# The last three output pairs of an attention kernel: another PSUM room, one sum on another engine, and two products in halves

## The chip, the cores and the metric

The kernel runs on one core of a Trainium2 chip. The metric is the device time of one execution in microseconds, as the median of several runs. PE is TensorE (PEld its weight loads), DVE is VectorE, ACT is ScalarE, POOL is GpSimd, SP is SyncE, which only issues DMAs here.

## The reference, cut to what matters

One multi-query attention layer over 64 blocks of 128 tokens, with a residual: layer norm, queries of 16 heads, one shared key and value, a bias and a causal and key mask, softmax, the output projection `Wo`, a second layer norm with gain `g_out`, and `x` added.

```python
B, H, N, DH, DIM = 64, 16, 128, 64, 512
xn   = layernorm(x, g_in)
q    = (xn @ Wq) -> [B, H, N, DH] * DH**-0.5
k, v = xn @ Wkv, each with a null row ahead
sim  = q @ k.T + bias, masked
out  = softmax(sim) @ v -> [B, N, H * DH]
out  = out @ Wo                      # 1024 -> 512
x    = x + layernorm(out, g_out)
```

All arithmetic is fp32.

## The kernel before, in words

The order of all instructions is written out by hand (`manual_schedule`); each engine has its own queue in that order, and semaphores for true dependencies are put in when the program is built. Blocks are handled in pairs. A step `d` makes the scores of blocks `a = 2d` and `b = 2d + 1`, takes the values and the output of the pair `p = 2d - 2, p + 1`, and normalises the pair before that, `l`.

The output projection of a pair is done with seven products instead of eight (a Strassen-like scheme over the two blocks and the two halves of `Wo`). `out_sum(p, k)` makes four sums of the transposed attention outputs `oT` (128 x 512 each): k = 0 writes the tile `yS`, the other three write over parts of `oT` in place. So sum 1 must wait until product 1 has read its operand, and sum 3 until product 2 has. `out_product(p, k, ...)` makes product k with 4 matmuls of 128 x 128 by 128 x 256 into one PSUM tile; products 6, 7 and 4 add to what product 1 left in its tile, product 3 to what product 5 left. `out_keep` copies a tile in between (`yp1`, `yu2`, `yp5`), `out_part` writes a half block of the output `ys` (256 columns).

Steps 1 to 29 are `turn` and `body`. The two steps ahead of the last pair, d = 30 and 31, are `turn_end` and `body_end`; `turn_end(32)` and `body_last` then finish the last pair, blocks 62 and 63, which has no scores beside it.

- `turn_end(d)`: scores of `a` and `b`, adding them to the bias (`scores_add`), maxima, the values of the pair `p` (`values`, tile `po`), ScalarE's exponentials of the first half of `a`, then `values_out_one`, which adds the null value and moves `po` to `oT`, ScalarE (L759) and VectorE (L757) in turn. The reciprocal `rinv(a, 0)` and the last `scores_add` follow on VectorE.
- `body_end(d)`: sums on GpSimd (L806), products on TensorE (L823) in the order 1, 2, 6, 5, 7, 3, 4, and among them the softmax of `a` and `b`: `scores_max`, `exps` (ScalarE), `rinv` (VectorE), `scale` (GpSimd, L664), `blocks_T` (VectorE transposes).
- `late_stats`, `pair_pow`, `late_nmr`, `late_norm`, `late_gain`, `late_residual` normalise a finished block: statistics on VectorE, the power -0.5 on GpSimd (L867), a scaling on ScalarE (L1037), the gain on VectorE (L1040), the residual on GpSimd (L1043), which also issues the store.
- `body_last`: products 1, 2, 5, 6, 3, 7, 4 of the last pair, and the normalisation of blocks 59 to 63. For block 62 VectorE subtracts the mean and multiplies by the gain (L1148) and then scales and adds the residual in one instruction (L1155). For block 63 `last_stats` reads product 4 out of PSUM.

PSUM has four kinds of room: `ps_s` "s" is one tile of two banks that the scores of `(a, 1)` use, `ps_q` "a" and "c", `ps_y` "X" and "Y", and `ps_w` "w" (two of it). Product 1 of a pair lies in "a" in `body_end`, and in "c" in `body_last`. The values `po` of the pair use "a", "w", "Y" and "w".

Of the kernel before, what the change touches and what calls it, by code (L numbers as in the profile page):

```python
# [17 lines left out]
def kernel(  # L18
# [63 lines left out]
    P = 128  # L82
# [593 lines left out]
    def blocks_T(b, lo=0, hi=R8):  # L676

        if lo == 0:
            sbs[b] = hp.tile([P, 6, R8, Q], FP, tag="sb", name=f"sb_{b}")
        nc.vector.transpose(  # L680
            sbs[b][:, :, lo:hi].rearrange("p j e q -> p e j q"),
            S[b][:, lo:hi, 1 : ROW - 1].rearrange("p e (j k) -> p e j k", k=Q),
        )
# [107 lines left out]
        p, m = ((e12, e11), (e22, wT[:, 0]), (e22, e12), (e21, wT[:, 1]))[k]  # L791
        nc.gpsimd.tensor_tensor(wT[:, k], p, m, ALU.subtract)

    def out_sum(p, k):

        h11, h12 = oT[p][:, 0], oT[p][:, 1]
        h21, h22 = oT[p + 1][:, 0], oT[p + 1][:, 1]
        if k == 0:
            yS[p] = bp.tile([P, HC, N], FP, tag="yS", name=f"yS_{p}", bufs=1)
        o, a, b, op = (  # L800
            (yS[p], h21, h22, ALU.add),
            (h11, yS[p], h11, ALU.subtract),
            (h21, h22, h11, ALU.subtract),
            (h12, h12, h11, ALU.subtract),
        )[k]
        nc.gpsimd.tensor_tensor(o, a, b, op)  # L806

    def out_product(p, k, pool, tag, start=True):
        key = "y" + tag
        if start:  # L810
            prod[key] = pool.tile([P, HE], FP, tag=tag, name=f"py{tag}_{p}_{k}")
        a, b = oT[p], oT[p + 1]
        h, w = {
            1: (a[:, 0], e11),
            2: (a[:, 1], e21),
            3: (a[:, 1], e22),
            4: (b[:, 1], wT[:, 3]),
            5: (yS.get(p), wT[:, 0]),
            6: (a[:, 0], wT[:, 1]),
            7: (b[:, 0], wT[:, 2]),  # L820
        }[k]
        for c in range(HC):
            nc.tensor.matmul(  # L823
                prod[key],
                h[:, c, :],
                w[:, c, :],
                start=(start and c == 0),
                stop=(c == HC - 1),
                skip_group_check=not start,
            )  # L830
# [8 lines left out]
    def out_part(b, e, tag, name=None):  # L839
        if b not in ys:  # L840
            if B - 6 <= b < B - 2:
                ys[b] = gp.tile(
                    [P, DIM], FP, tag=f"xS{b - B + 7}", name=f"y_{b}", bufs=1
                )
            elif b == B - 1:
                ys[b] = gp.tile([P, DIM], FP, tag="xT", name=f"y_{b}")
            else:
                ys[b] = hp.tile([P, DIM], FP, tag="y", name=f"y_{b}", bufs=3)
        o = ys[b][:, lo_e if e == 0 else hi_e]
        if name is None:  # L850
            nc.scalar.copy(o, prod["y" + tag])
        else:
            nc.vector.tensor_tensor(o, prod["y" + tag], kept.pop(name), ALU.add)
# [12 lines left out]
    def pair_pow(b):  # L866
        nc.gpsimd.tensor_tensor(yn[b][1], yn[b][1], nhalf, ALU.pow)  # L867
# [66 lines left out]
    def turn_end(d):  # L934

        a, b, p = 2 * d, 2 * d + 1, 2 * d - 2
        if d == PAIRS:
            blocks_T(*late_T.pop())
            late_gain(p - 4)
            late_residual(p - 4, nc.gpsimd)  # L940
            late_nmr(p - 3)
            values_rooms_apart(p)
            result_room(p)
            for m in (p, p + 1):
                values(m)
# [24 lines left out]
        scores_add(b, 1)  # L970

    def body_first():
# [66 lines left out]
    def late_gain(b):  # L1039
        nc.vector.tensor_tensor(ys[b], ys[b], gob, ALU.mult)  # L1040
# [5 lines left out]
    def body_end(d):  # L1046

        a, b, p, l = 2 * d, 2 * d + 1, 2 * d - 2, 2 * d - 4
        last = d + 1 == PAIRS
        lo, hi = (0, R8 // 2), (R8 // 2, R8)  # L1050
        for r in range(p, B if last else p + 2):
            load_res(r)
        out_sum(p, 0)
        scores_max(a, 1)
        late_stats(l if last else l + 1)
        out_product(p, 1, ps_q, "a")
        exps(b, 0, 0, 4)
        out_keep("a", "yp1", "yp1")
# [11 lines left out]
        out_keep("a", "yu2", "yu2")  # L1070
        exps(a, 1, *lo)
        rinv(a, 1, *lo)
        scale(a, 1, *lo)
        out_sum(p, 3)
        late_nmr(l)
        out_product(p, 5, ps_y, "Y")
        exps(a, 1, *hi)
        rinv(a, 1, *hi)
        scale(a, 1, *hi)
        out_keep("Y", "yp5", "yp5")  # L1080
        blocks_T(a, *lo)
        if last:
            late_stats(l + 1)
        else:
            late_nmr(l + 1)
        out_product(p, 7, ps_q, "a", start=False)
        exps(b, 1, *lo)
        out_part(p + 1, 1, "a", "yp5")
        rinv(b, 1, *lo)
        scale(b, 1, *lo)  # L1090
        blocks_T(a, *hi)
        out_product(p, 3, ps_y, "Y", start=False)
        exps(b, 1, *hi)
        rinv(b, 1, *hi)
        scale(b, 1, *hi)
        out_part(p, 1, "Y", "yu2")
        late_norm(l)
        if last:
            pair_pow(l + 1)
        else:  # L1100
            late_norm(l + 1)
        blocks_T(b, *lo)
        late_T.append((b, *hi))
        out_product(p, 4, ps_q, "a", start=False)
        out_part(p + 1, 0, "a")
        if not last:
            for m in (l, l + 1):
                late_gain(m)
                late_residual(m, nc.gpsimd)

    def body_last():
# [1 line left out]
        p = B - 2  # L1113
        y = p - 2
        st = [
            small.tile([P, 2, 6], FP, tag=f"stl{i}", name=f"stl{i}", bufs=1)
            for i in range(2)
        ]
# [28 lines left out]
        mv, rstd = last_stats(p, st[0], (1, ys[p][:, hi_e]))  # L1147
        nc.vector.scalar_tensor_tensor(  # L1148
            ys[p], ys[p], mv[:, 0:1], gob, ALU.subtract, ALU.mult
        )  # L1150
# [10 lines left out]
        y = ys[p + 1]  # L1161
# [374 lines left out]
```

## Time and profile before

| | us |
|---|---|
| median of 3 runs | 1038.36 |
| lowest and highest run | 1037.15, 1039.06 |
| the profiled execution's own time | 1036.99 |
| its span in the profile | 1035.2 |

The span runs from the first to the last recorded instruction of the profiled execution; the time of an execution also has 1.8 us around it. In the profile a row names line, engine, operation and tiles (out<-in). A bracket at the end of a timeline row says how long the engine sat idle before it and what ended that. Step 30 begins at 974.25 us of the span, step 31 at 993.73, and the last pair at 1013.24.

### The profile page before, as it was taken

The page shows a single profiled execution, that of the slowest core. Times are in us where ns is not written, and L with a number is a line of the kernel's source. Part 1 is how long each engine was busy: PE and PEld are TensorE (multiplying, and loading weights), DVE is VectorE, ACT ScalarE, POOL GpSimd, SP SyncE. Part 2 cuts the span into 40 slices and gives each one's busy share as a digit, 9 for nine tenths or more (in the row PEclk, how much of TensorE's full clock was granted, in tenths as well). Part 3 has the DMA queues.
Part 4 walks back from the last instruction along what each step waited for, and adds up shares of the span by engine and source line. Part 5 has one row for each costly group of instructions (what it writes and reads, how often), then busy time and mean ns, then how long its engine had stood idle before and what let it go on. Part 6 is the DMA issues. An engine that isn't in the chain of part 4 may idle for free.

```text
span 1035.2 us, 31163 instructions
## 1 busy us (share of the span) xinstructions
PE 1022.7 (99%) x12337; PEld 902.3 (87%) x12337; DVE 772.4 (75%) x1629; ACT 680.4 (66%) x2709; POOL 726.7 (70%) x540
## 2 busy tenths in 40 slices
PE   9999999999999999999999999999999999999997
PEld 8888888888888888888888888888888888888876
DVE  6776777876777877778777778767778777767687
ACT  4756677666677566686666776666776666856582
POOL 4897767676676767758667676776767677576686
PEclk9999999999999999999999999999999999999999
DMA  7514152241613315133151522415233151330211
GB/s 216 158 36 147 63 166 78 68 126 63 180 69 104 96 63 177 62 125 106 42 167 62 163 79 65 133 63 176 72 104 96 60 180 63 112 89 25 85 63 63
DMA packets 69226, 105.12 MB, mean 102 GB/s; under 512 B 9044, under 2 KB 33496, under 8 KB 67288
## 3 DMA queue, kind: packets, MB, share of 16 engines
q1 hardware_dynamic: 68640, 102.47, 31.7%
q8 instruction: 97, 1.59, 0.6%
q10 hardware_dynamic: 440, 0.66, 0.2%
q14 instruction: 49, 0.40, 0.1%
HBM read 67.45 MB, written 35.65 MB: 100 GB/s over the span
## 4 chain that ended last, share of the span: by engine, by line
PE 96%; POOL 2%; DMA 1%; issue 0%; DVE 0%; ACT 0%; ACTq 0%; POOLq 0%; DVEq 0%
PE pa L534 20%; PE pyX L823 19%; PE pyY L823 10%; PE pc L534 10%; PE po L740 8%; PE pkv L350 6%; PE pyw L823 5%; PE pw L534 5%; PE ps L611 3%; PE pq L469 3%; PE sc_X L611 2%; PE sc_Y L611 2%; PE sc_a L611 1%; POOL oT L806 1%; PE pya L823 1%; PE sc_w L611 1%
## 5 line engine op out<-in xcount | busy, mean ns | idle before, releaser
L642 ACT ACTIVATE s<-s,nmax 128x65 f32<-128x65 f32 (+1 forms) x1024 | 372.0, 367 | 59.0 <-DVE nmax L633 59.0
L664 POOL TENSOR_TENSOR s<-s,rinv 128x512 f32<-128x512 f32 (+1 forms) x132 | 190.8, 1447 | 166.0 <-DVE rinv L660 166.0
L576 POOL TENSOR_TENSOR s<-biasp,mneg 128x1552 f32<-128x1552 f32 (+1 forms) x65 | 206.0, 3172 | 41.2 <-DVE s L626 32.8
L642 ACT ACTIVATION_READ_ACCUMULATOR s<-s,nmax 128x1 f32 x1024 | 194.3, 190 | 0.0
L823 PE MATMUL pyX<-wT,oT 128*128 128x256 f32 x696 | 164.4, 379 | 0.0
L680 DVE STREAM_TRANSPOSE sb<-s 128x1536 f32<-128x1536 f32 (+1 forms) x68 | 114.1, 1678 | 61.5 <-POOL s L664 61.5
L823 PEld LDWEIGHTS pyX<-wT,oT 128*128 128x128 f32 x696 | 132.1, 190 | 18.1
L633 DVE TENSOR_REDUCE nmax<-s 128x8 f32<-128x1032 f32 (+1 forms) x128 | 121.4, 949 | 0.1
L534 PE MATMUL pa<-xS,wq 128*128 128x256 f32 x472 | 121.1, 379 | 0.0
L552 ACT COPY qT<-pa 128x256 f32<-128x256 f32 x59 | 22.0, 373 | 149.3 <-PE pa L534 149.2
L534 PEld LDWEIGHTS pa<-xS,wq 128*128 128x128 f32 x472 | 89.5, 190 | 12.3
L277 POOL TENSOR_TENSOR rstd<-rstd,nhalf 128x1 f32<-128x1 f32 x64 | 35.6, 557 | 77.2 <-DVE rstd L276 77.2
L806 POOL TENSOR_TENSOR oT<-oT 128x512 f32<-128x512 f32 x64 | 80.5, 1277 | 3.7 <-PE pyw L823 1.4
L740 PE MATMUL po<-sb,vr 32*64 32x256 f32 (+1 forms) x4008 | 81.4, 303 | 0.0
L740 PEld LDWEIGHTS po<-sb,vr 32*64 32x64 f32 x4008 | 71.2, 130 | 8.1 <-issue 5.7
L555 DVE TENSOR_TENSOR qT<-pc,ku 128x256 f32<-128x256 f32 x118 | 49.0, 415 | 38.5 <-ACT ku L546 21.3
L759 ACT ACTIVATE oT<-po,nv 128x512 f32<-128x512 f32 (+1 forms) x127 | 73.7, 654 | 1.2 <-PE po L740 1.1
L546 ACT COPY ku<-pa 128x256 f32<-128x256 f32 x118 | 43.9, 372 | 40.6 <-PE pa L534 37.4
L350 PE MATMUL pkv<-wkv,xT 128*128 128x128 f32 x512 | 65.2, 281 | 0.0
L350 PEld LDWEIGHTS pkv<-wkv,xT 128*128 128x128 f32 x512 | 59.6, 191 | 5.0 <-DVE s L626 4.8
L823 PE MATMUL pyY<-wo,oT 128*128 128x256 f32 x256 | 60.7, 380 | 1.1 <-POOL oT L806 1.1
L534 PE MATMUL pw<-xT,wq 128*128 128x256 f32 x240 | 61.4, 379 | 0.0
(163 smaller groups left out, 2260.0 us busy)
## 6 DMA issues: line engine op xcount, KB each, us to landing
res<-in_x_dram SPq DMA_DIRECT2D x64, 256.0 KB, 3.8
x<-in_x_dram SPq DMA_DIRECT2D x63, 256.0 KB, 8.2
out_dram<-y SPq DMA_DIRECT2D x63, 256.0 KB, 2.0
xd<-xb SPq DMA_DIRECT2D x14, 1024.0 KB
xT<-xd SPq DMA_DIRECT2D x56, 256.0 KB, 4.7
vr<-vd SPq DMA_DIRECT2D x64, 128.0 KB, 2.7
kT<-kd SPq DMA_DIRECT2D x64, 64.0 KB, 1.9
wo<-in_L_cond_Wo_dram SPq DMA_DIRECT2D x1, 2048.0 KB, 14.5
```

The source lines that it names most:

```text
L350: nc.tensor.matmul(pkv, xT[g][:, t, kc, :], wkv[:, kc, :], start=(kc == 0), stop=(kc == KC - 1),)
L534: nc.tensor.matmul(prod[tag], w[:, kc, f * P : (f + 1) * P], t[:, :, kc, :], start=(start and kc == 0), stop=(kc == HK - 1), skip_group_ch ...
L576: nc.gpsimd.tensor_tensor(S[b][:, :, keys], biasp[:, :, keys], mneg[:, t, keys] .unsqueeze(1) .broadcast_to([P, R8, keys.stop - keys.start ...
L611: nc.tensor.matmul(home[r][u * DH : (u + 1) * DH, f, :], qT[g, f, t // 2][rows, t % 2, hf, u], kT[g][rows, 0 : nk // Q, t, :], start=True, ...
L633: nc.vector.tensor_reduce(nmax[b][:, hf], S[b][:, :, WITH_NULL[hf]], AX.X, ALU.max, negate=True)
L642: nc.scalar.activation(row, row, AF.Exp, bias=nmax[b][:, hf, k : k + 1], accum_out=rsum[b][:, hf, k : k + 1],)
L664: nc.gpsimd.tensor_tensor(sv, sv, rinvs[b, hf][:, lo:hi].unsqueeze(2).broadcast_to([P, hi - lo, sv.shape[2]]), ALU.mult,)
L680: nc.vector.transpose(sbs[b][:, :, lo:hi].rearrange("p j e q -> p e j q"), S[b][:, lo:hi, 1 : ROW - 1].rearrange("p e (j k) -> p e j k", k=Q),
L740: nc.tensor.matmul(po[s][rows, to : to + n], vr[g][quad, j, t, :], sb[quad, slots, r * NF : (r + 1) * NF, :], start=(turn == 0), stop=True ...
L759: nc.scalar.activation(to, src, AF.Identity, bias=nv2)
L806: nc.gpsimd.tensor_tensor(o, a, b, op)
L823: nc.tensor.matmul(prod[key], h[:, c, :], w[:, c, :], start=(start and c == 0), stop=(c == HC - 1), skip_group_check=not start,)
```

## The change

In `body_end` (both steps) product 1 and what is added to it (products 6, 7 and 4) lie in the first half bank of the two-bank tile "s" instead of in "a". `out_sum(p, 0)` goes from GpSimd to VectorE and, with `scale(a, 0)`, from `body_end` to the end of `turn_end`, ahead of the last `scores_add`. So GpSimd has the scaling ahead of its sums 1, 2 and 3, where before it stood between sums 1 and 2.

In `turn_end(32)` the scale of block 59 on ScalarE (`late_norm(p - 3)`) goes ahead of the last pair's null adds, and its factor ahead of the gain of block 58.

In `body_last` the normalisations of blocks 59 to 61 stand in another order; the residual of block 59 goes from GpSimd to VectorE; block 62 is scaled by ScalarE and gets its residual from GpSimd instead of one VectorE instruction. Products 7 and 4 of the last pair are done in two halves of 128 columns each, with the add and the statistics in halves too. The statistics of block 63 have four groups of 128 columns instead of two of 256.

```diff
-    def out_sum(p, k):
+    def out_sum(p, k, eng=nc.gpsimd):
...
-        nc.gpsimd.tensor_tensor(o, a, b, op)
+        eng.tensor_tensor(o, a, b, op)
-    def out_product(p, k, pool, tag, start=True):
+    def out_product(p, k, pool, tag, start=True, cols=slice(0, HE)):
         key = "y" + tag
-        if start:
+        if start and pool is ps_s:
+            two = ps_s.tile([P, 2, DIM], FP, tag="s", name=f"py_{p}_{k}_s")
+            prod[key] = two[:, 0, 0:HE]
+        elif start:
             prod[key] = pool.tile([P, HE], FP, tag=tag, name=f"py{tag}_{p}_{k}")
...
-                prod[key],
+                prod[key][:, cols],
                 h[:, c, :],
-                w[:, c, :],
+                w[:, c, cols],
# turn_end
         if d == PAIRS:
             blocks_T(*late_T.pop())
+            late_nmr(p - 3)
+            late_norm(p - 3)
             late_gain(p - 4)
             late_residual(p - 4, nc.gpsimd)
-            late_nmr(p - 3)
...
-            late_norm(p - 3)
             return
...
         rinv(a, 0)
+        scale(a, 0)
+        out_sum(p, 0, nc.vector)
         scores_add(b, 1)
# body_end
-        out_sum(p, 0)
         scores_max(a, 1)
         late_stats(l if last else l + 1)
-        out_product(p, 1, ps_q, "a")
+        out_product(p, 1, ps_s, "s")
...
-        scale(a, 0)
...
-        out_product(p, 6, ps_q, "a", start=False)
+        out_product(p, 6, ps_s, "s", start=False)
...
# body_last
         out_sum(p, 0)
         late_stats(y)
+        late_gain(y - 1)
         out_product(p, 1, ps_q, "c")
         out_keep("c", "yp1", "yp1")
+        pair_pow(y)
         out_sum(p, 1)
-        late_gain(y - 1)
+        late_nmr(y)
+        late_norm(y)
         late_stats(y + 1)
-        pair_pow(y)
-        pair_pow(y + 1)
         out_product(p, 2, ps_w, "w")
         out_part(p, 0, "w", "yp1")
         nc.vector.bn_stats(st[0][:, 0], ys[p][:, lo_e])
+        pair_pow(y + 1)
         out_sum(p, 3)
         out_product(p, 5, ps_y, "Y")
-        late_nmr(y)
+        late_nmr(y + 1)
+        late_gain(y)
         out_keep("Y", "yp5", "yp5")
         out_sum(p, 2)
+        late_norm(y + 1)
+        late_residual(y - 1, nc.vector)
         out_product(p, 6, ps_q, "c", start=False)
-        late_nmr(y + 1)
         out_keep("c", "yu2", "yu2")
-        late_norm(y)
-        late_norm(y + 1)
-        late_residual(y - 1, nc.gpsimd)
-        late_gain(y)
         late_residual(y, nc.gpsimd)
+        late_gain(y + 1)
         out_product(p, 3, ps_y, "Y", start=False)
-        late_gain(y + 1)
         out_part(p, 1, "Y", "yu2")
+        late_residual(y + 1, nc.gpsimd)
         mv, rstd = last_stats(p, st[0], (1, ys[p][:, hi_e]))
+        def upper(part):
+            out_product(p, 7, ps_q, "c", start=False, cols=part)
+            nc.vector.tensor_tensor(
+                y[:, hi_e][:, part], prod["yc"][:, part], k5[:, part], ALU.add
+            )
+            nc.vector.bn_stats(st[1][:, parts.index(part)], y[:, hi_e][:, part])
+        upper(parts[0])
         nc.vector.scalar_tensor_tensor(
             ys[p], ys[p], mv[:, 0:1], gob, ALU.subtract, ALU.mult
         )
-        late_residual(y + 1, nc.gpsimd)
-        out_product(p, 7, ps_q, "c", start=False)
-        out_part(p + 1, 1, "c", "yp5")
-        nc.vector.bn_stats(st[1][:, 1], ys[p + 1][:, hi_e])
-        nc.vector.scalar_tensor_tensor(
-            ys[p], ys[p], rstd, res.pop(p), ALU.mult, ALU.add
-        )
-        store(p)
-        out_product(p, 4, ps_q, "c", start=False)
+        nc.scalar.activation(ys[p], ys[p], AF.Copy, scale=rstd)
+        upper(parts[1])
+        late_residual(p, nc.gpsimd)
         x0 = prod["yc"]
-        mv, rstd = last_stats(p + 1, st[1], (0, x0))
+        for i, part in enumerate(parts):
+            out_product(p, 4, ps_q, "c", start=False, cols=part)
+            if i == 0:
+                nc.vector.bn_stats(st[1][:, 2], x0[:, part])
+        mv, rstd = last_stats(p + 1, st[1], (3, x0[:, parts[1]]))
```

More of the change, by code (lines that the diff above doesn't have):

```diff
@@ L844, in out_part @@
                 )
-            elif b == B - 1:
-                ys[b] = gp.tile([P, DIM], FP, tag="xT", name=f"y_{b}")
             else:
@@ L1085, in body_end @@
             late_nmr(l + 1)
-        out_product(p, 7, ps_q, "a", start=False)
+        out_product(p, 7, ps_s, "s", start=False)
         exps(b, 1, *lo)
-        out_part(p + 1, 1, "a", "yp5")
+        out_part(p + 1, 1, "s", "yp5")
         rinv(b, 1, *lo)
@@ L1103, in body_end @@
         late_T.append((b, *hi))
-        out_product(p, 4, ps_q, "a", start=False)
-        out_part(p + 1, 0, "a")
+        out_product(p, 4, ps_s, "s", start=False)
+        out_part(p + 1, 0, "s")
         if not last:
@@ L1115, in body_last @@
         st = [
-            small.tile([P, 2, 6], FP, tag=f"stl{i}", name=f"stl{i}", bufs=1)
+            small.tile([P, 2 + 2 * i, 6], FP, tag=f"stl{i}", name=f"stl{i}", bufs=1)
             for i in range(2)
@@ L1130, in body_last @@
         nc.vector.bn_stats(st[0][:, 0], ys[p][:, lo_e])
+        pair_pow(y + 1)
         out_sum(p, 3)
         out_product(p, 5, ps_y, "Y")
-        late_nmr(y)
+        late_nmr(y + 1)
+        late_gain(y)
         out_keep("Y", "yp5", "yp5")
         out_sum(p, 2)
+        late_norm(y + 1)
+        late_residual(y - 1, nc.vector)
         out_product(p, 6, ps_q, "c", start=False)
-        late_nmr(y + 1)
         out_keep("c", "yu2", "yu2")
-        late_norm(y)
-        late_norm(y + 1)
-        late_residual(y - 1, nc.gpsimd)
-        late_gain(y)
         late_residual(y, nc.gpsimd)
+        late_gain(y + 1)
         out_product(p, 3, ps_y, "Y", start=False)
-        late_gain(y + 1)
         out_part(p, 1, "Y", "yu2")
+        late_residual(y + 1, nc.gpsimd)
         mv, rstd = last_stats(p, st[0], (1, ys[p][:, hi_e]))
+        parts = slice(0, HE // 2), slice(HE // 2, HE)
+        y = ys[p + 1] = gp.tile([P, DIM], FP, tag="xT", name=f"y_{p + 1}")
+        k5 = kept.pop("yp5")
+        def upper(part):
[5 more added lines that the diff above has]
+        upper(parts[0])
         nc.vector.scalar_tensor_tensor(
```

5 lines of the change are left out of this document (2 added, 3 removed).

## The prediction

> **What bounds the kernel now.** I read the page first: its busy times and its chain of waits.
>
> ```profile
> PE 1022.7 (99%) x12337; PEld 902.3 (87%) x12337; DVE 772.4 (75%) x1629; ACT 680.4 (66%) x2709; POOL 726.7 (70%) x540
> PE 96%; POOL 2%; DMA 1%; issue 0%; DVE 0%; ACT 0%; ACTq 0%; POOLq 0%; DVEq 0%
> ```
>
> TensorE is the bound: busy for 99% of the span and 96% of the chain. The change gives it no less work, so it can win only where TensorE waits. It touches only the two `body_end` steps (pairs 60/61 and 62/63 in the scores, output pairs 58/59 and 60/61) and `body_last` (output pair 62/63). The busy times by stretch of these three:
>
> ```profile
> 974.25:993.73 19.48, 17.93 (x313) 15.27 (x312) 15.14 (x34) 15.60 (x73) 17.14 (x14) 1.00 0.01 2
> 993.73:1013.24 19.51, 18.14 (x314) 15.47 (x313) 17.57 (x39) 14.89 (x72) 14.88 (x14) 1.00 0.25 83
> 1013.24:1035.20 21.96, 15.07 (x185) 12.67 (x184) 16.25 (x36) 5.02 (x10) 13.58 (x13) 0.95 0.20 74
> ```
>
> The columns are the window, its length, then PE, PEld, DVE, ACT and POOL. PE is idle for 1.55, 1.37 and 6.89 us; that is all there is to win. The timeline of PE says in front of which product (the fifth row's product comes straight behind another, for comparison; the sixth ends the last pair's five whole products):
>
> ```profile
> 980.61 1.99 PE L823 MATMUL pya<-wo,oT 128*128 128x256 f32 x8 [0.99 <-ACT oT L759]
> 990.08 1.99 PE L823 MATMUL pyY<-wo,oT 128*128 128x256 f32 x8 [0.55 <-POOL oT L806]
> 1000.12 1.99 PE L823 MATMUL pya<-wo,oT 128*128 128x256 f32 x8 [0.83 <-DVE oT L757]
> 1027.93 1.99 PE L823 MATMUL pyc<-wT,oT 128*128 128x256 f32 x8 [1.62 <-DVE y L853]
> 984.17 1.91 PE L823 MATMUL pya<-wT,oT 128*128 128x256 f32 x8
> 1022.70 1.89 PE L823 MATMUL pyY<-wo,oT 128*128 128x256 f32 x8
> ```
>
> Product 1 waits for the null adds, product 3 for GpSimd's last sum, and the last pair's product 4 for VectorE, which reads product 7 late.
>
> **Part 1, the two steps ahead.** The chain of waits in the first of them, in order of time:
>
> ```profile
> 979.75 0.82 ACT oT L759 x2
> 982.75 1.28 POOL oT L806
> 984.03 1.00 POOL s L664
> 985.03 1.24 POOL oT L806
> 986.27 0.51 POOL lrs L867
> 986.78 2.02 POOL s L664 x2
> 988.80 1.24 POOL oT L806
> ```
>
> Product 1 waited for two null adds because its room "a" was also read by the second. In the scores' tile only the first binds it: half of 0.82, so 0.4 us earlier, at 980.2. The new room is read last by `scores_add(a, 1)`, long done. Afterwards it holds the next `scores(a, 1)` until ScalarE has copied product 4; two score groups come first on PE and hide that, and without them it would cost the copy, 0.4 us.
>
> On GpSimd the first sum leaves (it was off the chain), and `scale(a, 0)`, 1.00 here, moves ahead of the second sum. That second sum waited for product 1, so the scaling now has to end before 982.35 to be free. VectorE's rows around it:
>
> ```profile
> 981.17 0.19 DVE L660 RECIPROCAL rinv<-rsum 128x8 f32<-128x8 f32 x1
> 981.28 0.64 DVE L626 TENSOR_TENSOR s<-sc_c,s 128x512 f32<-128x512 f32 x1
> 986.46 0.17 DVE L660 RECIPROCAL rinv<-rsum 128x4 f32<-128x4 f32 x1
> ```
>
> `rinv(a, 0)` ends at 981.36, and the new VectorE sum stands right behind it at 981.28. No row shows that sum on VectorE. It reads two tensors in SBUF, like the gain multiply of L1040, of the same shape. What such an instruction does beside GpSimd is the second thing to read:
>
> ```profile
> 1013.79 0.65 DVE L1040 TENSOR_TENSOR y<-y,gob 128x512 f32<-128x512 f32 x1
> 1016.84 1.27 POOL L806 TENSOR_TENSOR yS<-oT 128x512 f32<-128x512 f32 x1 [1.05 <-ACT oT L759]
> 1017.57 1.09 DVE L1040 TENSOR_TENSOR y<-y,gob 128x512 f32<-128x512 f32 x1
> 1018.19 1.60 POOL L806 TENSOR_TENSOR oT<-yS,oT 128x512 f32<-128x512 f32 x1
> 1023.24 1.82 DVE L1040 TENSOR_TENSOR y<-y,gob 128x512 f32<-128x512 f32 x1
> 1023.24 1.27 POOL L1043 TENSOR_TENSOR y<-y,res 128x512 f32<-128x512 f32 x1
> 42.16 2.13 POOL L516 TENSOR_TENSOR xS<-xT,xS 128x512 f32<-128x512 f32 x1
> 43.20 2.18 DVE L502 TENSOR_TENSOR wS<-wS,wq 128x1024 f32<-128x1024 f32 x1
> 44.26 2.88 POOL L664 TENSOR_TENSOR s<-s,rinv 128x1024 f32<-128x1024 f32 x1
> ```
>
> Alone the multiply takes 0.65; against a running GpSimd instruction it takes 1.09 and 1.82, and GpSimd's 1.27 becomes 1.60 the other way round. They take turns: from the ends of the rows, VectorE's work begins about 0.11 before GpSimd's recorded end, and GpSimd's about 0.14 before VectorE's. The last three rows show who is next: VectorE, waiting from 43.20, ends at 45.38, ahead of the scaling of 44.26.
>
> The Trainium skill, SBUF — State Buffer, section Who interferes with whom, has it as a rule against this change: a VectorE instruction with two SBUF inputs and a GpSimd instruction that reads SBUF exclude each other for a whole instruction, and whichever issues first goes first. The trace agrees (1.82 against 0.65). By overlap without exclusion, the sum would come out as the first rival below.
>
> So VectorE's sum runs from 981.28 to 981.93, the scaling from 981.8 to 982.8, and the second sum starts at 982.8, where it started at 982.75. Product 6, which waits for it, gains nothing: it starts at about 984.2, and PE's idle time has only moved behind product 2. Behind it GpSimd is shorter by the scaling, 1.00, but VectorE is later by the sum, 0.58 from start to start. The second `rinv` moves from 986.46 to about 987.1, and the next scaling with it. Second sum, third, power, a scaling, 0.4 of waiting, a scaling and the fourth sum make 1.24 + 1.24 + 0.51 + 1.01 + 0.4 + 1.01 + 1.24 = 6.65, so the fourth ends at 989.5 instead of 990.04. PE, restarted at 984.2, needs 0.1 + 3 x 1.73 and comes there at 989.5 too (984.17 to 985.9 and so on is the spacing of 1.73). Product 3 gains 0.3 to 0.5 of its 0.55. The second step repeats this. Since VectorE is its busiest there (17.57 of 19.51), I take the lower end there and a little above it in the first: **0.75 us earlier** into `body_last`, with bounds of 0.4 and 1.1.
>
> **Part 2, the last pair up to `out_part(p, 1)`.** All of part 1's gain has to pass through VectorE. Up to the gain of block 59 nothing new binds; `late_norm(59)` moved ahead of the null adds on ScalarE ends before product 1 can start, as TensorE is still in the values of block 63. Then VectorE waits for the power of block 60, which now stands ahead of the second sum on GpSimd: some 0.45 idle, where statistics ran before. What follows is three VectorE instructions with two SBUF inputs (gain 60, the residual of 59 taken from GpSimd, gain 61) against three on GpSimd (fourth sum, third sum, residual 60). By the rows above a turn of both takes 1.27 + 0.65 - 0.25 = 1.67. GpSimd's first begins at 1016.1 + 1.27 (first sum) + 1.0 (power, held by gain 59) + 1.24 + 0.52 + gaps, about 1020.4. Three turns end at 1025.4. The next rows are VectorE's way to the end as it was:
>
> ```profile
> 1025.58 0.41 DVE L853 TENSOR_TENSOR y<-pyY,kyu 128x256 f32<-128x256 f32 x1
> 1026.03 0.43 DVE L1177 BATCH_NORM_STATS2 stl<-y 128x6 f32<-128x256 f32 x1
> 1026.73 0.15 DVE L1181 TENSOR_SCALAR rstdo<-mvo 128x1 f32<-128x1 f32 x1
> 1026.80 0.74 DVE L1148 SCALAR_TENSOR_TENSOR y<-y,mvo,gob 128x512 f32<-128x512 f32 x1
> 1027.46 0.42 DVE L853 TENSOR_TENSOR y<-pyc,kyp 128x256 f32<-128x256 f32 x1
> 1029.97 0.43 DVE L1177 BATCH_NORM_STATS2 stl<-pyc 128x6 f32<-128x256 f32 x1 [0.23 <-PE pyc L823]
> ```
>
> `out_part(p, 1)` stood at 1025.58 and comes at about 1025.45: of the 0.75, **0.1 us** is left here (bounds: -0.5, none of it lost before this point but one turn more; 1.7, no turns at all and the product of 1022.70 + 1.89, 0.75 earlier, as the only wait).
>
> **Part 3, the halves.** From `out_part(p, 1)` to the last statistics took 1029.97 - 1025.58 = 4.39. In the order of the built program each half product carries a wait on VectorE, and the two halves lie in one PSUM tile. The second half of product 7 waits for the add that reads the first half, product 4's first half for the other add, its second half for the statistics of the first. They alternate with VectorE and do not overlap it. The prices of 128 columns:
>
> ```profile
> 948.09 2.05 PE L350 MATMUL pkv<-wkv,xT 128*128 128x128 f32 x16
> L350 PE MATMUL pkv<-wkv,xT 128*128 128x128 f32 x512 | 65.2, 281 | 0.0
> L385 DVE TENSOR_TENSOR kvt<-pkv,nkv 128x128 f32<-128x128 f32 x2 | 0.5, 281 | 0.0
> ```
>
> Sixteen such matmuls are spaced (2.05 - 0.28) / 15 = 0.118, so a half product is 7 x 0.118 + 0.28 + 0.1 (restart, 1.99 against 1.89) = 1.21; with 0.04 to be seen, 1.25. The add is 0.28. No row has statistics of 128 columns: between 0.28 (the add) and 0.43 (256 columns); I take 0.30. With 0.05 for each signal back: 1.22 to the first add (where 1026.80 stood), 0.33, 1.25, 0.33, 1.25, 0.35, 1.25 = 5.98. That is **1.6 us more** (bounds 1.3, if a half is half of 1.99 + 0.1; 1.9). The subtract of block 62 (0.74) now fits beside a half. ScalarE's scaling and GpSimd's residual of block 62 replace a VectorE instruction that was covered by product 4; they end some 2 us before the last power is asked for and cost nothing. Should they be later than that, the power would wait for what remains of 1.27.
>
> The Trainium skill, PSUM — Partial Sum Buffer, section PSUM bank collisions raise a hardware error, speaks against the halves: TensorE's writing and VectorE's reading are to be kept apart by bank, not by address, even at disjoint columns. No run here shows a collision; the waits of the built program are what one would place by that rule. Guarded by columns instead, the last statistics would come about 1.9 us sooner.
>
> **Sum.** Behind the last statistics all is as before, less 0.13 for 128 instead of 256 columns. -0.1 + 1.6 - 0.1 = +1.4, and reckoned through each engine's queue in order with the same durations +1.3, which I take. The profiled execution took 1036.99 us; 1.3 more is 1038.3. It lies 1.37 below the median of the runs, 1038.36, on which I put the same difference: **1039.7 us**. A measurement of this kernel can tell about 0.2%, 2.1 us, from no change.
>
> **Rivals.** *First: the turns of part 2 do not form*, because sums and gains fall into each other's gaps. For it: in the second step VectorE's transposes and GpSimd ran side by side. Against: GpSimd has no gap between 1020.4 and 1025. `out_part(p, 1)` would come at 1023.84, 1.74 earlier: -1.74 + 1.6 - 0.13 = -0.3, or 1038.1; with part 1 at its bound of 1.1, 1037.7. Chance 0.16.
> *Second, on the slower side: the VectorE sum loses the port to `scale(a, 0)`.* The two are released by the same reciprocal; VectorE is ahead only while its queue brings the sum within some 0.1 us of 981.28, and it also waits for ScalarE's null add. From there on the sum starts behind the scaling, 0.95 later, and the adds, maxima and `rinv` behind it, so the fourth sum and product 3 too. One step: 1.3 + 0.95 = 2.25, 1040.6; both: 1041.6. Against: ScalarE's add is done 0.3 us before. Chance 0.22.
>
> **Numbers.** The forecast has 0.60; its own range, from the bounds of parts 1 to 3 and some 0.7 us of scatter in a median, is 1038.8 to 1041.0, a quarter of it beyond 1040.44. The remaining 0.02 lie near no change. Slower: 0.15 + 0.21 = 0.36. Faster than 1036.28: only a part of the first rival, 0.04. Within: 0.60. The range takes in both rivals: 1037.6 to 1041.7.
>
> **What would show it.** In the profile after: in both steps an idle PE ahead of product 6 instead of product 3; VectorE's L806 at about 0.65 with a GpSimd L664 stretched behind it; in `body_last` gains and residuals of 1.4 to 1.8; four half products of 1.1 to 1.2 with VectorE between them. It is wrong if `out_part(p, 1)` comes before 1024.5, if the halves stand back to back, or if L806 on VectorE takes over 1.2.

## The result, and the profile after

The changed kernel takes 1039.43 us (median of 22 runs, 1037.85 to 1041.89). The kernel before, run 22 times beside it, takes 1037.51 us (1037.04 to 1039.06), so the three runs shown ahead of the prediction lay 0.85 too high. The ratio is 1.0016, with a 95% interval of 1.0009 to 1.0022: slower by 0.16%, some 1.7 us (the two medians are 1.92 apart). The interval lies clear of no change; the loss is inside the 0.2% that the prediction called no change. The profiled execution took 1040.03 us, with a span of 1038.2, 3.0 more than that of before; it is one of the longer ones.

The page's busy times and chain of waits, after:

```profile
PE 1025.4 (99%) x12353; PEld 904.2 (87%) x12353; DVE 774.3 (75%) x1634; ACT 681.2 (66%) x2710; POOL 724.7 (70%) x538
PE 95%; DVE 2%; POOL 1%; DMA 1%; issue 1%; ACT 0%; ACTq 0%; POOLq 0%; DVEq 0%
```

TensorE is still the bound, yet its busy time rose by 2.7 us without any added work (the 16 matmuls more are halves of whole ones). The busy times by stretch say where:

```profile
974.25:993.73 19.48, 18.63 (x316) 15.52 (x314) 15.90 (x36) 15.59 (x73) 16.88 (x13) 1.00 0.01 2
993.73:1013.24 19.51, 18.69 (x322) 15.56 (x328) 18.37 (x40) 14.96 (x73) 14.15 (x13) 1.00 0.24 84
1013.24:1038.20 24.96, 17.19 (x200) 14.72 (x198) 17.33 (x39) 5.82 (x11) 13.62 (x12) 0.89 0.17 64
```

In the two steps TensorE is idle for 0.85 and 0.82 us, where it was 1.55 and 1.37: the first half of the change did its work. In the last stretch it is busy for 17.19 instead of 15.07, and the granted clock, the column behind POOL, is 0.89 instead of 0.95. TensorE's timeline, product by product (six rows of the steps, the last pair's first product, the four halves):

```profile
980.87 1.99 PE L826 MATMUL py_s<-wo,oT 128*128 128x256 f32 x8 [0.64 <-ACT oT L759]
984.73 1.99 PE L826 MATMUL py_s<-wT,oT 128*128 128x256 f32 x8
990.25 1.99 PE L826 MATMUL pyY<-wo,oT 128*128 128x256 f32 x8
1000.04 1.97 PE L826 MATMUL py_s<-wo,oT 128*128 128x256 f32 x8 [0.54 <-ACT oT L759]
1003.93 1.99 PE L826 MATMUL py_s<-wT,oT 128*128 128x256 f32 x8 [0.20 <-POOL oT L806]
1009.45 1.99 PE L826 MATMUL pyY<-wo,oT 128*128 128x256 f32 x8
1015.56 1.99 PE L826 MATMUL pyc<-wo,oT 128*128 128x256 f32 x8
1024.76 1.13 PE L826 MATMUL pyc<-wT,oT 128*128 128x128 f32 x8 [0.30 <-DVE kyu L838]
1027.48 1.16 PE L826 MATMUL pyc<-wT,oT 128*128 128x128 f32 x8 [1.59 <-DVE y L1156]
1029.02 1.99 PE L826 MATMUL pyc<-wT,oT 128*128 128x128 f32 x8 [0.38 <-DVE y L1156]
1031.40 1.70 PE L826 MATMUL pyc<-wT,oT 128*128 128x128 f32 x8 [0.39 <-DVE stl L1172]
```

Product 1 waits less, product 3 hardly at all, and product 6 waits now. The four halves alternate with VectorE, as forecast. But the same eight matmuls took 1.13 and 1.16 as product 7 and 1.99 and 1.70 as product 4. Three windows, ahead of those last two halves, over them and behind:

```profile
1025.70:1029.10 3.40, 1.43 (x11) 1.05 (x9) 2.96 (x10) 0.61 (x1) 1.77 (x2) 1.00 0.47 175
1029.10:1032.50 3.40, 3.01 (x13) 2.71 (x14) 0.49 (x2) 0.11 (x1) 1.27 (x1) 0.51 0.21 77
1032.50:1033.10 0.60, 0.60 (x5) 0.40 (x4) 0.00 (x0) 0.00 (x0) 0.00 (x0) 0.95 0.00 0
```

After 3.4 us in which TensorE was busy for 1.43, its clock was halved for 3.4 us, and both halves of product 4 fell into that. VectorE and GpSimd in the two steps and in the last pair:

```profile
981.89 0.64 DVE L806 TENSOR_TENSOR yS<-oT 128x512 f32<-128x512 f32 x1
982.05 1.39 POOL L664 TENSOR_TENSOR s<-s,rinv 128x512 f32<-128x512 f32 x1 [1.67 <-DVE rinv L660]
983.40 1.27 POOL L806 TENSOR_TENSOR oT<-yS,oT 128x512 f32<-128x512 f32 x1
988.92 1.27 POOL L806 TENSOR_TENSOR oT<-oT 128x512 f32<-128x512 f32 x1
1001.10 0.64 DVE L806 TENSOR_TENSOR yS<-oT 128x512 f32<-128x512 f32 x1
1001.26 1.39 POOL L664 TENSOR_TENSOR s<-s,rinv 128x512 f32<-128x512 f32 x1 [4.11 <-DVE rinv L660]
...
1021.06 1.54 DVE L1043 TENSOR_TENSOR y<-y,gob 128x512 f32<-128x512 f32 x1
1022.52 1.75 DVE L1046 TENSOR_TENSOR y<-y,res 128x512 f32<-128x512 f32 x1
1024.54 1.41 DVE L1043 TENSOR_TENSOR y<-y,gob 128x512 f32<-128x512 f32 x1
1025.87 0.41 DVE L854 TENSOR_TENSOR y<-pyY,kyu 128x256 f32<-128x256 f32 x1
1033.13 0.30 DVE L1188 BATCH_NORM_STATS2 stl<-pyc 128x6 f32<-128x128 f32 x1 [1.79 <-PE pyc L826]
```

To compare executions I count from the first of the bias adds ahead of the two steps (the row that starts at 969.71 before), since what lies ahead of it is the same code and still moved by 0.6 us (970.32 after); where an expectation speaks of the last bias add, this row is meant:

```profile
970.32 3.20 POOL L576 TENSOR_TENSOR s<-biasp,mneg 128x1552 f32<-128x1552 f32 x1
```

The starts in the profiled executions, behind that row, of the last pair's product 1, of `out_part(p, 1)` and of the last statistics, and the end of VectorE's last instruction; then the medians, that of before being the one on the same chip (a ratio is not exactly that of its two medians):

| kernel | product 1 | out_part(p, 1) | last statistics | end | median us | before | ratio (95%) |
|---|---|---|---|---|---|---|---|
| before | 45.97 | 55.87 | 60.26 | 62.83 | | 1037.51 | |
| after | 45.24 | 55.55 | 62.81 | 65.31 | 1039.43 | 1037.51 | 1.0016 (1.0009 to 1.0022) |
| e1_whole | 45.24 | 55.56 | 59.33 | 62.10 | 1036.65 | 1037.62 | 0.9990 (0.9981 to 0.9999) |
| e2_halves | 46.01 | 55.91 | 61.80 | 64.30 | 1038.86 | 1037.95 | 1.0013 (1.0004 to 1.0022) |
| e3_steps | 45.22 | 55.12 | 59.50 | 62.08 | 1036.98 | 1037.62 | 0.9995 (0.9986 to 1.0003) |
| e4_fill | 45.51 | 55.83 | 62.54 | 65.04 | 1039.46 | 1037.62 | 1.0017 (1.0009 to 1.0026) |
| e5_banks | 45.51 | 55.84 | 59.82 | 62.32 | 1036.64 | 1037.62 | 0.9992 (0.9983 to 1.0001) |
| e6_fill6 | 45.25 | 55.57 | 61.46 | 63.96 | 1038.59 | 1037.95 | 1.0009 (1.0000 to 1.0017) |
| e7_addfirst | 45.23 | 55.12 | 59.59 | 62.16 | 1036.69 | 1037.95 | 0.9990 (0.9981 to 0.9999) |
| e8_room | 46.01 | 55.89 | 60.27 | 62.85 | 1036.96 | 1037.60 | 0.9993 (0.9984 to 1.0002) |
| e9_res59 | 45.50 | 54.44 | 58.68 | 62.48 | 1036.53 | 1037.95 | 0.9986 (0.9977 to 0.9995) |
| e10_best | 45.24 | 54.18 | 58.42 | 61.20 | 1035.51 | 1037.60 | 0.9978 (0.9969 to 0.9988) |
| e11_sum | 45.75 | 55.63 | 60.01 | 62.59 | 1036.56 | 1037.60 | 0.9991 (0.9982 to 1.0000) |

From `out_part(p, 1)` to the last statistics: 4.38 before, 7.26 after.

### The profile page after: what moved, and what is told of

It is laid out like the page before. It is cut to its first block, busy times and chain, and to the rows that moved or that the text cites. A ratio compares the mean times of both kernels' runs of the same rounds, so it can differ in the third digit from the quotient of the medians.

```text
span 1038.2 us, 31205 instructions
## 1 busy us (share of the span) xinstructions
PE 1025.4 (99%) x12353; PEld 904.2 (87%) x12353; DVE 774.3 (75%) x1634; ACT 681.2 (66%) x2710; POOL 724.7 (70%) x538
## 4 chain that ended last, share of the span: by engine, by line
PE 95%; DVE 2%; POOL 1%; DMA 1%; issue 1%; ACT 0%; ACTq 0%; POOLq 0%; DVEq 0%
PE pa L534 20%; PE pyX L826 19%; PE pyY L826 10%; PE pc L534 10%; PE po L740 8%; PE pkv L350 6%; PE pw L534 5%; PE pyw L826 5%; PE ps L611 3%; PE pq L469 3%; PE sc_X L611 2%; PE sc_Y L611 2%; PE sc_a L611 1%; PE sc_w L611 1%; DMA wq<-in_L_cond_Wq_dram 1%
## 5 line engine op out<-in xcount | busy, mean ns | idle before, releaser
L534 PE MATMUL pc<-xT,wS 128*128 128x256 f32 x236 | 60.7, 379 | 0.2 <-DVE qT L555 0.2
```

The lines of the kernel that those rows point to most:

```text
L534: nc.tensor.matmul(prod[tag], w[:, kc, f * P : (f + 1) * P], t[:, :, kc, :], start=(start and kc == 0), stop=(kc == HK - 1), skip_group_ch ...
```

## The experiments

**e1_whole: the halves undone.**

```
-        parts = slice(0, HE // 2), slice(HE // 2, HE)
+        parts = (slice(0, HE),)
...
-        upper(parts[1])
...
-            if i == 0:
-                nc.vector.bn_stats(st[1][:, 2], x0[:, part])
-        mv, rstd = last_stats(p + 1, st[1], (3, x0[:, parts[1]]))
+        mv, rstd = last_stats(p + 1, st[1], (1, x0))
```

> The changed kernel with products 7 and 4 of the last pair whole again (256 columns), their add still ahead of the subtract of block 62; the rest of the change stays. Theory one (the halves alternate with VectorE and are the whole loss): from out_part(p,1) at 0 the statistics, their sum and rstd take 1.26, the add 0.41, product 4 runs from 1.75 to 3.74, the last statistics begin at 3.85 instead of 7.26 in the changed kernel and 4.39 in the kernel before; with the 0.3 us that out_part(p,1) comes earlier the kernel is 0.9 us faster than before, about 1036.6 us where before is 1037.5. Rival (the new order of gains, residuals and powers in body_last is the loss, the halves cost nothing): about 1039.4 us, as with the change. Rival two (only the dropped clock in the last two halves costs): about 1038.0 us.

`out_part(p, 1)` stays where the change put it (55.56), and the last statistics follow after 3.77 (expected 3.85) instead of 7.26. The median is 1036.65, under that of before. The halves are more than the whole loss; the rival that blames the new order is out, and so is the one that blames the clock alone (1038.0). The stretch is shorter than before's 4.38 because product 4 starts 0.61 sooner (1.74 behind `out_part(p, 1)` in place of 2.35), as VectorE adds product 7 ahead of the subtract of block 62. e7_addfirst below shows that this order alone is not enough: there product 4 starts as early, but block 62's last step is still VectorE's and delays the statistics.

**e2_halves: the halves alone, in the kernel before.** Products 7 and 4 as in the change, everything else as before:

```
-        out_product(p, 7, ps_q, "c", start=False)
-        out_part(p + 1, 1, "c", "yp5")
-        nc.vector.bn_stats(st[1][:, 1], ys[p + 1][:, hi_e])
+        upper(parts[0])                 # ahead of the subtract of block 62
...
+        upper(parts[1])
```

> The kernel before with only the last pair's products 7 and 4 in halves of 128 columns; the two steps, the order of gains and residuals and the work on block 62 as before. Theory one (halves alternate with VectorE; a halved clock, where it falls there, comes on top): from out_part(p,1) to the last statistics 5.9 us at full clock and up to 7.2 with the clock halved, instead of 4.38; 1.3 to 2.6 us slower, 1039.0 us in the median where before is 1037.6. Rival (the halves cost only together with the rest of the new last pair): at most 0.3 us slower, 1037.9 us.

5.89 from `out_part(p, 1)` to the last statistics, 1.51 more than before, and 0.9 us slower in the median (1.3 by the ratio). The four halves stand as in the change, and none takes over 1.16:

```profile
1024.81 1.05 PE L826 MATMUL pyc<-wT,oT 128*128 128x128 f32 x8
1027.57 1.16 PE L826 MATMUL pyc<-wT,oT 128*128 128x128 f32 x8 [1.71 <-DVE y L1158]
1029.11 1.16 PE L826 MATMUL pyc<-wT,oT 128*128 128x128 f32 x8 [0.38 <-DVE y L1158]
1030.66 1.16 PE L826 MATMUL pyc<-wT,oT 128*128 128x128 f32 x8 [0.39 <-DVE stl L1177]
```

So the alternation is one cost, and the clock another, which this execution did not pay.

**e4_fill and e6_fill6: TensorE kept busy in its waits.** Matmuls of 128 columns that nobody reads, into a free PSUM tile; e6_fill6 has 6, 1 and 1 of them in place of 12, 2 and 2:

```
         upper(parts[0])
+        fill(12)
...
         upper(parts[1])
+        fill(2)
...
                 nc.vector.bn_stats(st[1][:, 2], x0[:, part])
+                fill(2)
```

> The changed kernel with products that nobody reads in TensorE's waits: 12 of 128 columns behind the first half of product 7, 2 behind its second half and 2 behind the first half of product 4, into a PSUM tile that is free. Theory one (the clock was halved for 3.4 us because TensorE was idle between the halves): the granted clock stays at 1.0, the last two halves take 1.1 to 1.2 instead of 1.99 and 1.70, the last statistics come 1.2 us sooner in the profile, and the median is 0.5 to 1.2 us below the changed kernel's, 1038.2 to 1038.9 us. Rival (the two halves were slow because GpSimd's residual and VectorE's reads disturb them): they still take 1.7 to 2.0 and the median stays at 1039.4 us or, by the added work, a little above.

> As e4_fill, with 6, 1 and 1 of the unread products instead of 12, 2 and 2, so that they end before the add that TensorE waits for (they took 2.6 us for 12). Theory one (clock): granted clock 1.0 throughout, the second half of product 7 starts where the add ends, 0.9 us earlier than with 12; from out_part(p,1) to the last statistics 5.8 to 5.98 us, and the median is 0.9 us below that of e4_fill, 1038.5 us. Rival (with less filling the activity is too low and the clock drops all the same): 1.99 and 1.70 us for the last halves, 7.2 us from out_part(p,1) to the last statistics, 1039.4 us.

TensorE's timeline of e4_fill (two rows), then of e6_fill6 from the first half on:

```profile
1025.65 2.84 PE L1157 MATMUL spare<-wT,oT 128*128 128x128 f32 x24
1028.33 1.06 PE L826 MATMUL pyc<-wT,oT 128*128 128x128 f32 x8
```

```profile
1026.00 1.13 PE L826 MATMUL pyc<-wT,oT 128*128 128x128 f32 x8 [0.30 <-DVE kyu L838]
1026.97 1.50 PE L1157 MATMUL spare<-wT,oT 128*128 128x128 f32 x12
1028.73 1.16 PE L826 MATMUL pyc<-wT,oT 128*128 128x128 f32 x8 [0.25 <-DVE y L1167]
1030.27 1.16 PE L826 MATMUL pyc<-wT,oT 128*128 128x128 f32 x8 [0.16 <-DVE y L1167]
1031.82 1.16 PE L826 MATMUL pyc<-wT,oT 128*128 128x128 f32 x8 [0.17 <-DVE stl L1185]
```

In both the clock stayed at 1.00 up to the end of the last half, and all halves took 1.06 to 1.16; the rival that blames the other engines' reads is out. In e4_fill the fill ran on for 2.84 us and held the second half back by some 0.9 (counted from `out_part(p, 1)`), so its median (1039.46) missed what was expected. In e6_fill6 it ended in time: 5.89 to the last statistics, as in e2_halves, and 1038.59, as expected. The 1.37 between 7.26 and 5.89 is the clock's. In the medians the gain (1.0016 to 1.0009) lies within the intervals' overlap, and e2_halves kept its clock without any fill, so one profile of each does not prove that the fill held it.

The record settles more, since it has the mean granted clock of each execution, from which 3.4 us at half take 0.0016. It is 0.997 or less in 7 of the 22 executions of the changed kernel and in 1 of 11 of e2_halves, and in none of the 199 others that have a clock on record, 22 of them filled. (0.998 can also come from a fall behind the last product, as in the profile of e6_fill6.) It is 0.999 in 5 of the 22, too high for a whole window at half. The median time of these five is 1038.69, that of the seven 1040.03: 1.34 apart, as the 1.37 of the profiles. So the clock falls in some executions of the alternating halves and not in others.

**e5_banks: the second halves in a bank of their own.**

```
+        tags = "ca"
...
-            out_product(p, 7, ps_q, "c", start=False, cols=part)
+            i = parts.index(part)
+            out_product(p, 7, ps_q, tags[i], start=False, cols=part, first=i == 1)
...
```

> The changed kernel with the second halves of products 7 and 4 in a PSUM tile of their own (another bank) instead of the other half of the same tile; nothing else moves. It leaves out the earlier product's share in those 128 columns (the second half starts from zero). Theory one (the waits between the halves are there because both lie in one bank): the second half of product 7 runs straight behind the first, product 4's first half waits only for the first add, and the last statistics come 1.6 us sooner than with alternating halves at full clock, 2.9 sooner than in the profile of the change; 1036.5 to 1037.8 us. Rival (VectorE's own row of adds and statistics of 128 columns is the bound): at most 0.5 us sooner, 1038.9 us.

```profile
1024.13 1.13 PE L826 MATMUL pyc<-wT,oT 128*128 128x128 f32 x8 [0.32 <-DVE kyu L838]
1025.10 1.06 PE L826 MATMUL pya_hi<-wT,oT 128*128 128x128 f32 x8
1026.86 1.16 PE L826 MATMUL pyc<-wT,oT 128*128 128x128 f32 x8 [0.70 <-DVE y L1159]
1028.04 1.16 PE L826 MATMUL pya_hi<-wT,oT 128*128 128x128 f32 x8
```

The second half of product 7 stands straight behind the first, and 3.98 instead of 5.89 pass up to the last statistics: 1.9 sooner, the figure that the prediction gave for waits by columns. Lying in one tile, and so in one bank, is what made the halves alternate; no run has two tiles in one bank, so tile and bank are not told apart. Even so the halves are no quicker than whole products in e1_whole (3.77).

**e3_steps, e8_room, e11_sum: the two steps.** e3_steps has both edits of the steps on the kernel before; e8_room only the room, e11_sum only the sum and the scaling:

```
+        scale(a, 0)                     # e3_steps, e11_sum
+        out_sum(p, 0, nc.vector)        # e3_steps, e11_sum
...
-        out_product(p, 1, ps_q, "a")
+        out_product(p, 1, ps_s, "s")    # e3_steps, e8_room
```

> The kernel before with only the two steps ahead changed (product room in the scores' two-bank tile, first sum on VectorE, first scaling earlier); the last pair as before, in its old order and with whole products. Theory one: product 1 of the last pair starts 0.7 to 0.75 us earlier and, the last pair's VectorE and GpSimd queues being those of before, 0.5 to 0.75 of it reaches the end: 1036.8 to 1037.0 us where before is 1037.5. Rival (VectorE's own queue in the last pair gives it back, since the gains and statistics there do not start earlier): product 1 is earlier but out_part(p,1) is not, 1037.5 us.

> The kernel before with only the products' room in the two steps moved into the scores' two-bank tile; the first sum stays on GpSimd and the first scaling behind the second sum. Theory one (product 1 waits for one null add less, and every sum behind it on GpSimd moves with it, since the first sum ends ahead of product 1): product 1 of the first step 0.35 us earlier, product 3 of it 0.35 to 0.4, product 1 of the second step 0.65 and of the last pair 0.65 us earlier, counted from the last bias add ahead of the steps; about 0.6 us faster than before. Rival (GpSimd's chain from its first sum on, not product 1, sets product 3): product 3 does not move and the last pair starts 0.0 to 0.1 us earlier; as before.

> The kernel before with only the first sum of the two steps on VectorE and the first scaling ahead of the second sum; the products' room stays "a". Theory one (GpSimd's chain behind product 1 is shorter by the scaling and later by VectorE's stalls): product 1 of the first step as before, product 3 of it 0.4 us earlier, product 1 of the second step 0.4 and of the last pair 0.75 to 0.8 us earlier, as with the room moved as well: then the room's gain only moves idle time to product 6. Rival (both edits are needed, each takes its own wait away): the last pair 0.3 to 0.45 us earlier.

Starts behind the bias add:

| kernel | product 1, step 1 | product 6 | product 3 | product 1, step 2 | product 3 | product 1, last pair |
|---|---|---|---|---|---|---|
| before | 10.90 | 14.46 | 20.37 | 30.41 | 39.87 | 45.97 |
| e8_room | 10.54 | 14.10 | 20.01 | 30.44 | 39.91 | 46.01 |
| e11_sum | 10.89 | 14.45 | 19.92 | 30.51 | 39.65 | 45.75 |
| e3_steps | 10.54 | 14.40 | 19.92 | 29.71 | 39.12 | 45.22 |
| after | 10.55 | 14.41 | 19.93 | 29.72 | 39.13 | 45.24 |

e3_steps brings 0.75 to the last pair, and all of it reaches the end (62.83 to 62.08) in the profile; the median fell by 0.64, its interval reaching just past 1. In the first step each edit alone does what was expected of it (product 3 0.36 and 0.45 earlier), and together they give 0.45, not 0.81: the room's gain ends as a wait of product 6. Then e8_room and e11_sum lost it again in the values of the second step, which took 3.39 and 3.21 us in place of 2.65, and the last pair came 0.04 later and 0.22 earlier, where 0.65 and 0.75 to 0.8 earlier had been expected. In e8_room TensorE stood still in them with nothing to wait for that the trace shows:

```profile
998.36 0.48 PE L740 MATMUL po<-sb,vr 32*64 32x256 f32 x13 [0.26 <-issue]
```

No expectation had that. It is no mark of the single edits: e4_fill, e5_banks and e9_res59 have the steps of the change, which took 2.76 there, but took 3.03 and began the last pair 0.27 later. The medians of the single edits (0.64 and 1.04 us under before) do not fit a lost gain either, so whether they bring less than both together is open.

**e7_addfirst: e3_steps with the add of product 7 ahead of the subtract of block 62.**

```
-        nc.vector.scalar_tensor_tensor(
-            ys[p], ys[p], mv[:, 0:1], gob, ALU.subtract, ALU.mult
-        )
...
         nc.vector.bn_stats(st[1][:, 1], ys[p + 1][:, hi_e])
+        nc.vector.scalar_tensor_tensor(
+            ys[p], ys[p], mv[:, 0:1], gob, ALU.subtract, ALU.mult
+        )
```

> e3_steps (the kernel before with the two steps changed) with one edit in the last pair: VectorE adds product 7 before the subtract of block 62, not behind it. Theory one (product 4 waits for that add and for nothing else): out_part(p,1) as in e3_steps, the add 0.65 us earlier, from out_part(p,1) to the last statistics 3.77 us as in e1_whole instead of 4.38, all of which reaches the end: 0.75 + 0.6 = 1.35 us faster than before, 1036.25 us. Rival (the subtract and the multiply of block 62 then come behind product 4's end and delay the last statistics): 3.77 + 0.4, 1036.6 us or more.

The rival came in the profile: 4.47, not 3.77. VectorE's subtract fell beside GpSimd's residual of block 61 and took 1.65 where it took 0.74 before; the scaling behind it ended after product 4:

```profile
1027.20 1.65 DVE L1155 SCALAR_TENSOR_TENSOR y<-y,mvo,gob 128x512 f32<-128x512 f32 x1
1027.04 1.26 POOL L1048 TENSOR_TENSOR y<-y,res 128x512 f32<-128x512 f32 x1
```

The median lies 1.26 under before, close to theory one's 1.35 and lower than that of e3_steps (0.64), but the intervals of the two ratios overlap, so the times do not decide it.

**e9_res59 and e10_best: fewer turns on VectorE.** e9_res59 is e1_whole with block 59's residual back on GpSimd; e10_best also has block 61's residual on VectorE, behind the subtract of block 62:

```
-        late_residual(y - 1, nc.vector)
+        late_residual(y - 1, nc.gpsimd)     # e9_res59, e10_best
...
-        late_residual(y + 1, nc.gpsimd)     # e10_best
...
+        late_residual(y0 + 1, nc.vector)    # e10_best, ahead of the scaling of block 62
```

> e1_whole (the change with whole products) with one edit: the residual of block 59 is added by GpSimd, as in the kernel before, and not by VectorE. Theory one (out_part(p,1) is late because VectorE's gains and that residual, 0.65 alone, take 1.4 to 1.75 each in turns with GpSimd): VectorE has one turn less, out_part(p,1) comes 1.2 us earlier than in e1_whole and waits for product 3 only, product 7 runs straight behind product 3, and the last statistics come 0.9 us sooner: 1035.8 us. Rival one (GpSimd, with one instruction more, delays the residual of 61 and the power of block 62 by 1.3 to 1.7 and with them the end): 1036.6 us, as e1_whole, or later. Rival two (a turn is bound by GpSimd's own sums, which do not move): out_part(p,1) less than 0.3 us earlier, 1036.4 us.

> e9_res59 (the change with whole products and the residual of block 59 on GpSimd) with one edit: the residual of block 61 is added by VectorE, behind the subtract of block 62, so that GpSimd comes to the power of block 62 1.3 us sooner. Theory one (in e9_res59 the last power waited 1.27 us behind GpSimd's residuals): out_part(p,1) and the last statistics as in e9_res59, 54.4 and 58.7 us behind the last bias add ahead of the steps, the subtract of block 62 takes 0.74 instead of 1.39, the last power comes 0.9 to 1.0 us sooner, and the kernel is 1.2 to 1.4 us faster than before (1036.3 where before is 1037.6). Rival (the residual on VectorE takes turns with GpSimd's residual of block 62 and delays the last statistics): no gain against e9_res59 or a loss of up to 0.7 us.

In e9_res59 `out_part(p, 1)` came 1.12 earlier than in e1_whole, behind product 3 alone: the turns were the delay. But rival one came too: GpSimd, with one instruction more, came late to the last power, and VectorE waited for that:

```profile
1025.54 0.42 DVE L854 TENSOR_TENSOR y<-pyY,kyu 128x256 f32<-128x256 f32 x1 [0.21 <-PE pyY L826]
1032.70 0.88 DVE L1177 SCALAR_TENSOR_TENSOR y<-y,rstdo,res 128x256 f32<-128x256 f32 x2 [1.27 <-POOL rstdo L1190]
```

e10_best takes that wait away: the subtract takes 0.73, the residual 0.69, and the end comes 1.02 sooner behind `out_part(p, 1)` (7.01 in place of 8.04; the rest of the 1.28 between the ends in the table is the later start of e9_res59). It is 2.1 us faster than before, more than the 1.2 to 1.4 expected, and the only kernel here whose ratio lies beyond 0.2% (its interval reaches from 0.12 to 0.31%):

```profile
1026.75 0.73 DVE L1161 SCALAR_TENSOR_TENSOR y<-y,mvo,gob 128x512 f32<-128x512 f32 x1
1027.40 0.69 DVE L1046 TENSOR_TENSOR y<-y,res 128x512 f32<-128x512 f32 x1
1030.36 0.88 DVE L1177 SCALAR_TENSOR_TENSOR y<-y,rstdo,res 128x256 f32<-128x256 f32 x2
```

## Why the prediction was right, and where it was not

The time (1039.7 for 1039.43) and the kind (no change) came out; the range, which took in both rivals, would have held for either. In the profiled executions, counted from the bias add, the sum was this:

| term | forecast | measured | from |
|---|---|---|---|
| the two steps | -0.75 | -0.74 | product 1 of the last pair |
| the turns in the last pair take back | +0.65 | +0.41 | `out_part(p, 1)`, -0.32 left |
| the halves, at full clock | +1.6 | +1.51 | e2_halves, e6_fill6 |
| the halved clock | none | +1.37 | after, 7.26 against 5.89 |
| behind the last statistics | -0.13 | -0.08 | 2.58 to 2.50 |
| sum | +1.3 to +1.4 | +2.48 | end, 62.83 to 65.31 |

- **Part 1** held in its steps. Product 1 came 0.35 earlier (0.4). VectorE's sum took 0.64 (0.65) and stretched the scaling to 1.39, so that the second sum started at 982.79 on before's scale (982.8). Product 6 gained nothing, and product 3 came 0.44 earlier (0.3 to 0.5).
- **Part 2**: the turns formed, at 1.54, 1.75 and 1.41 where 1.67 was reckoned for each; 0.32 instead of 0.1 was left. e9_res59 shows that they bind. The first rival is out with that.
- **Part 3** held in mechanism and price at full clock: halves of 1.05 to 1.16 (1.21), adds of 0.29 (0.28), statistics of 0.30 (0.30), 5.89 for 5.98, and e5_banks gave the 1.9 named for unguarded columns. The step that failed is a term of this sum: product 4's halves, priced at 1.21 each and measured at 1.99 and 1.70; the upper bound of 1.9 for this part was passed (2.88). The working priced the half at the clock of a busy TensorE and put it behind three pauses. The 0.95 in the last window of before was quoted and not followed up; there the clock fell behind the last product (0.70 from 1032 to 1035), where it cost nothing.
- **The second rival** did not come: in both steps VectorE's sum took 0.64.
- **The base**: 1.3 was put on a median of three runs that lay 0.85 too high. The medians are 1.92 apart, 0.6 more than the 1.3, as the clock falls in part of the executions only. The missing clock and the high base have opposite signs, and the close hit of 0.3 us is luck in that.

The Trainium skill, TensorE: Matmul & The Clock Gate, section What's actually happening, says that the clock goes to half after an idle window of about 3.4 us and that the window runs freely, not from the kernel's start. The trace agrees with the halving (0.51) and the length (3.4 us) and differs in the condition: TensorE was busy for 1.43 of the 3.40 us ahead of it and never idle for over 1.6. That the window runs freely the kept traces bear out: in all 13 the record of the granted clock begins at 4.4 to 11.0 us of the span, at 1.00, and the clock first falls 300, 301 or 302 times 3.413 us later, so no product of the last pair sets where a window begins. In e2_halves the two windows on that grid held 1.71 and 2.40 us of work, and the clock stayed:

```profile
1025.23:1028.65 3.42, 1.71 (x14) 1.41 (x12) 3.13 (x9) 0.00 (x0) 2.95 (x3) 1.00 0.38 148
1028.65:1032.06 3.41, 2.40 (x17) 1.94 (x16) 1.87 (x5) 0.00 (x0) 0.97 (x1) 1.00 0.42 159
```

Over an edge between the two, a stretch of the same length held only 1.32 and cost nothing. In the 13 traces the clock fell behind every window with 0 to 1.44 us of work and behind one with 1.69 (e6_fill6, after its last product), and stayed behind one with 1.57 (e9_res59) and all with 1.71 or more. Up to the end of its last product, e6_fill6 has no stretch of 3.41 us with less than 2.83, and the kernel before none with less than 1.79. So the pauses between halves make a fall possible, and where the windows' edges lie in an execution decides whether it comes.

## What to carry to other kernels

Splitting a product so that another engine can start on its first half cost 1.51 us here while both halves lay in one PSUM tile: each half was a full round trip (1.16 + 0.38), and the pauses can cost the clock as well (1.37). With a tile for each half they no longer alternated, but still brought nothing over whole products in the same order (3.98 against 3.77). When an instruction with two SBUF inputs is moved between VectorE and GpSimd, count the turns in the new place, 1.4 to 1.75 for one of 0.65, and look at what is queued behind it on both engines: e9_res59 gained 1.1 us on one and lost it on the other. A wait that goes is best followed to the next instruction that waits, in the same step, before its gain is added to another's.

## What had not been expected of the hardware

- The granted clock fell to 0.5 for 3.4 us though TensorE had been busy for 42% of the 3.4 us before (1.43 of 3.40). The falls of all 13 traces lie on a grid of 3.413 us, and a window with 1.57 or 1.71 us of work left the clock at 1.00.
- In the values of the second step TensorE's instructions spanned 2.65 to 3.39 us from kernel to kernel, with a pause (0.26 put down to issue in e8_room) for which the trace shows no wait.
- VectorE's subtract of two SBUF tensors with a per-row scalar takes turns with GpSimd as the gain multiply does: 0.73 alone, 1.65 beside a residual (e10_best, e7_addfirst).
